# Layer 1 of a four-layer graph network: the copy of the attention weights becomes a job of its own and moves ahead of the norm and the scatters, and the attention product moves ahead of the aggregation

## The chip, the cores and the metric

The kernel runs on one core of one Trainium2 chip. The metric is device time in microseconds (us). Three runs of the kernel before gave 2053.06, 2053.97 and 2055.26 us; 2053.97 is their median.

## What is computed

The input `x` is 128 graphs of 64 nodes with 256 features; `adj` is one 64x64 adjacency matrix that all graphs share. Four graph layers follow one another. Each is added to its input and normalised over the features:

```python
x = _layernorm(x + _L0(x, adj, W, a))
x = _layernorm(x + _L1(x, W_lin, W_val, a, W_out, adj, src, dst))
x = _layernorm(x + _L2(x, adj, W1, b1, g1, be1, W2, b2, g2, be2))
x = _layernorm(x + _L3(x, adj, Wg0, bg0, Wg1, bg1, Wih, Whh, bih, bhh))
```

The change sits in the second half of layer 1 and in the first operation of layer 2. They are, in short:

```python
# layer 1: attention along 512 edges (src -> dst), 4 heads of 64
Xq = (H @ W_lin.T).reshape(bt, n, h, dh)
Xv = (H @ W_val.T).reshape(bt, n, h, dh)
e = einsum('behd,hd->beh', leaky_relu(Xq[:, src] + Xq[:, dst], 0.2), a)
e = e + log(A0[src, dst] + EPS)
ex = exp(e - segment_max(e, src)[src])        # softmax over the edges of one src
attn = ex / segment_sum(ex, src)[src]
Y = segment_sum(attn * Xv[:, dst], src)
return Y @ W_out.T
# layer 2
agg = einsum('nm,bmd->bnd', A_hat, features)  # A_hat: adjacency, scaled by degrees
h = relu(batchnorm(agg @ W1.T + b1))          # statistics over all 8192 rows
return batchnorm(h @ W2.T + b2)
```

Layer 0 is a graph attention with a dense 64x64 softmax. Layer 3 has two graph convolutions and then four LSTMs; it takes the larger part of the time, and the change doesn't touch it.

## The kernel before

**Tiling.** The 8192 rows are cut into NQ = 16 blocks of 512 rows, which is eight graphs or PQ = 4 chunks of 128 rows (two graphs each). A block stays on the chip in a tile `A` from layer to layer.

**The loop of layer 1.** It runs over `q` from 0 to 15. Each step is cut into eight sub-steps `b`. A sub-step starts with `l1_graph`, which is one graph: the product L355 forms queries plus keys on the 512 edges in `z`, and ScalarE's L357 copies them to `u` with a relu. After it come the jobs that the table `between` lists for this sub-step. They belong to neighbouring blocks:

- Layer 0 of the blocks q+1 and q+2 (`l0_a` to `l0_e`). The change's neighbours in it are ScalarE's copy of the transposed attention `eT` (L285) and the product L293, which has eight weight loads and reads `eT`.
- `l1_t` and `l1_qv`: the transposes, the query product (L318), the value product (L321), and the copies out of their banks. ScalarE's L328 copies `qs`, VectorE's L329 subtracts for the other half, ScalarE's L330 copies to `spad`, and ScalarE's L331 copies the values `v`.
- `sums`: the reduction over heads (L346), which reads `u`.
- The softmax of a pair of blocks, numbered S, every second step. `l1_softmax` runs L365 to L375 with the exponential L374, and `l1_sums` holds the two scans L380 and L381. `l1_weights` transposes (L389), normalises (L397), writes the weights with four scatters of GpSimd's into a table in memory (L401), and loads the table back as `ld` with two DMAs on SyncE's queue.
- `v_a` of a block LAG = 3 steps back. GpSimd's copy L414 sorts the weights of this block out of `ld` into `am`. Then comes the attention product L422, 64 matmuls of 64x64, and two copies of ScalarE's (L426) empty its banks into `yT`.
- `v_b`: the output product L436, the residual sum of VectorE's (L438), the layernorm, and a store of the result. In the layernorm, VectorE takes statistics (L95, L96) and adds the epsilon (L85), GpSimd raises to the power -1/2 (L86), VectorE negates the mean (L98), and GpSimd scales the four chunks (L100).
- `v_c`: the aggregation of layer 2 (L456, 64 matmuls of 64x64 on the normalised rows) and the copy into `A` (L460 in the loop, two L463 after it).

**What sets the order.** In the loop the helper `step` chains only TensorE's instructions of successive jobs. All other engines get an order from a scheduler, which places what is ready. After the loop the helper `given` holds every job behind the one before it on TensorE, VectorE, ScalarE and GpSimd alike. Each engine works through its queue in the order that was built.

**Buffers.** A PSUM bank comes from `bank`: three of the name `m` go round among most products, two are `z`, one is `e`. The tiles `am`, `ld`, `y`, `at` and `yT` have one buffer each, so a new one waits for the last reader of the old one. `v` has five buffers.

**The end of layer 1.** After the loop the blocks 12 to 15 are still under way. The list `fill` holds pieces of layer 2's first product (`up_block`, with the matmuls L749, ScalarE's L754 and VectorE's statistics L755; later pairs of blocks with L820). A piece is put after every job `v_a`, `v_b` and `v_c`. The last softmax (S = 7) belongs to the blocks 14 and 15: its `l1_softmax` comes right after the loop, its `l1_sums` and `l1_weights` among the first pieces.

Of the kernel before, what the change touches and what calls it, by code (L numbers as in the profile page):

```python
# [8 lines left out]
F32 = mybir.dt.float32  # L9
# [8 lines left out]
P = 128  # L18
NB = 128
N = 64  # L20
D = 256
KD = D // P
HEADS = 4
# [3 lines left out]
NQ = 16  # L27
PQ = 4
# [13 lines left out]
def kernel(ctx: ExitStack, tc: tile.TileContext, i, out):  # L42
# [67 lines left out]
    def given(do, *args, **more):  # L110
        traced = nc.cur_bb.bb.instructions
        first = len(traced)
        with ExitStack() as order:
            for e in latest.values():
                order.enter_context(tc.issue_after(e))
            r = do(*args, **more)  # L116
        for t in traced[first:]:
            if t.engine in (mybir.EngineType.PE, mybir.EngineType.DVE, mybir.EngineType.Activation,
                            mybir.EngineType.Pool):
                latest[t.engine] = t  # L120
        return r
# [8 lines left out]
    with ExitStack() as two:  # L130
# [7 lines left out]
        vp = values.enter_context(tc.tile_pool(name="vp", bufs=1, side="right"))  # L138
# [5 lines left out]
        def bank(shape, name="m", bufs=3):  # L144
            return (psm if name == "m" else ps).tile([P] + shape, F32, name=name, bufs=bufs)
# [158 lines left out]
        L1 = {}  # L304
# [102 lines left out]
                nc.sync.dma_start(ld[S][s * N:(s + 1) * N], half)  # L407


        def v_a(q):  # L410
            S, b = divmod(q, BPS)
            v = L1[q]["v"]
            am = vp.tile([P, PQ * HEADS, N], F32, name="am")
            nc.gpsimd.tensor_copy(am.rearrange("p (e r) n -> p e r n", e=2),  # L414
                                  ld[S].rearrange("p n (e b r) -> p b e r n", e=2, b=BPS)[:, b])
            pY = [bank([KD, PQ, N]) for _ in range(2)]
            for c in range(PQ):
                for h in range(HEADS):
                    for s in range(2):
                        r = slice(s * N, (s + 1) * N)  # L420
                        r0 = (h % 2) * 64
                        nc.tensor.matmul(pY[s][r0:r0 + 64, h // 2, c, :], v[r, c, h * 64:(h + 1) * 64],  # L422
                                         am[r, (c % 2) * 2 * HEADS + c // 2 * HEADS + h, :], start=True, stop=True)
            yT = L1[q]["yT"] = vp.tile([P, KD, PQ, 2, N], F32, name="yT")
            for s in range(2):
                nc.scalar.activation(yT[:, :, :, s, :], pY[s], AF.Copy)  # L426
# [234 lines left out]
        LAG = BPS + 1  # L661
# [4 lines left out]
        def step(do, n, *more):  # L666
            if not 0 <= n < NQ:
                return
            traced = nc.cur_bb.bb.instructions
            first = len(traced)  # L670
            if queue:
                with tc.issue_after(queue[-1]):
                    do(n, *more)
            else:
                do(n, *more)
            mine = [t for t in traced[first:] if t.engine == mybir.EngineType.PE]
            queue.extend(mine[-1:])
# [4 lines left out]
        for q in range(NQ):  # L682
            S = q // BPS - 1 if q % BPS == 0 else -1
            between = [
                [(l0_e, q + 1), (l0_a, q + 2)],
                [(sums, q if q else -1), (l1_softmax, S)],
                [(l1_sums, S), (l0_b, q + 2)],
                [(v_b, q - LAG - 1)],
                [(l1_weights, S), (l1_t, q + 1), (l0_c, q + 2)],
                [(sums, q), (l1_qv, q + 1, 0)],  # L690
                [(v_c, q - LAG - 1), (v_a, q - LAG)],
                [(l0_d, q + 2), (l1_qv, q + 1, 1)],
            ]
            for b in range(GQ):
                step(l1_graph, q, b)
                for do, n, *more in between[b]:
                    step(do, n, *more)
                if setup:
                    setup.pop(0)()
        sums(q)  # L700
        S = NQ // BPS - 1
# [55 lines left out]
        def up_block(q):  # L757
            for m in range(2):
                put(q, m, up(q, m))
                if m == 0:  # L760
                    last_tail()
            pz = [up(q, m) for m in (2, 3)]
            for m in (2, 3):
                put(q, m, pz[m - 2])
# [134 lines left out]
        def tile_sums(b):  # L899

            t2, t3, t4 = rooms[next(rooms_at) % len(rooms)]
            t1 = b(0, 1)
            given(nc.gpsimd.tensor_tensor, t3, b(1, 1), t1, OP.subtract)
            given(nc.vector.tensor_sub, t1, t1, b(0, 0))
            given(nc.gpsimd.tensor_tensor, t2, b(1, 1), t1, OP.subtract)
            given(nc.gpsimd.tensor_tensor, t4, b(1, 0), t2, OP.subtract)
            return [t1, t2, t3, t4]
# [12 lines left out]
        def inputs(q):  # L920
            return lambda k, n: Aq(q + n)[:, k * QT:(k + 1) * QT]

        def up_job(q, g, T, done=None, feed=iter(()), **more):
            a = lambda m, k: w1[:, k, (2 * g + m) * P:(2 * g + m + 1) * P]
            dst = lambda m, n: hidden(q + n, 2 * g + m)
            stats = lambda m, n: nc.vector.bn_stats(st1[:, 2 * g + m, q + n, :], dst(m, n))
            seven(Seven([(a, [SW[0][:, n, g] for n in range(4)], inputs(q), T)],
                        lambda m: b1[:, 2 * g + m:2 * g + m + 1], dst, stats, done, **more), feed)
# [3 lines left out]
        def one(q):  # L932
            return lambda: up_block(q)

        def pair(q, g):
            return lambda: up_job(q, g, T[q])

        fill = [one(n) for n in range(7)] + [pair(n, g) for n in (7, 9) for g in range(2)]
        given(v_b, NQ - LAG - 1)
        fill.pop(0)()  # L940
        given(l1_sums, S)
        fill.pop(0)()
        given(v_c, NQ - LAG - 1, False)
        given(l1_weights, S)
        sums_at = {3: 7, 5: 9}
        for n, (do, q) in enumerate([(do, q) for q in range(NQ - LAG, NQ) for do in (v_a, v_b, v_c)]):
            given(do, q, *[False] * (do == v_c))
            fill[n]()
            if n in sums_at:
                T[sums_at[n]] = tile_sums(inputs(sums_at[n]))  # L950
        q = NQ - LAST - 1
# [1023 lines left out]
```

## Time and profile before

| what | value |
|---|---|
| median of three runs | 2053.97 us (2053.06 to 2055.26) |
| profiled execution | 2051.53 us, of which its span is 2049.7 us |
| granted TensorE clock, mean | 0.986 |
| 0 to 155 us | TensorE busy 125.81 |
| 155 to 520 us (365.0) | TensorE 342.48, ScalarE 239.62, VectorE 212.96, GpSimd 136.50 |
| 520 to 620 us (100.0) | TensorE 95.51, VectorE 54.88, GpSimd 43.59, ScalarE 35.68 |
| 620 to 2049.7 us (1429.7) | TensorE 1379.77, VectorE 895.54, GpSimd 672.64, ScalarE 625.24 |

The profile is one execution, recorded by the hardware. Its span reaches from the first to the last instruction; the execution's own time is a little longer. The engines are PE (TensorE's matmuls), PEld (its weight loads), DVE (VectorE), ACT (ScalarE), POOL (GpSimd) and SP (SyncE, which issues DMAs). A line of the timeline gives start, length, engine, program line, operation, and output and input tiles with shapes; a bracket at its end says how long the engine had been idle and which instruction ended that. A line of the waits gives the waiting tile and line, the instruction that released it, the total, how often, and the longest. The four stretches of the table are the start with layer 0, the loop with softmax and attention, the end of layer 1, and layers 2 and 3.

### The profile page before, as it was taken

The page shows a single profiled execution, that of the slowest core. Times are in us where ns is not written, and L with a number is a line of the kernel's source. Part 1 is how long each engine was busy: PE and PEld are TensorE (multiplying, and loading weights), DVE is VectorE, ACT ScalarE, POOL GpSimd, SP SyncE. Part 2 cuts the span into 40 slices and gives each one's busy share as a digit, 9 for nine tenths or more (in the row PEclk, how much of TensorE's full clock was granted, in tenths as well). Part 3 has the DMA queues.
Part 4 walks back from the last instruction along what each step waited for, and adds up shares of the span by engine and source line. Part 5 has one row for each costly group of instructions (what it writes and reads, how often), then busy time and mean ns, then how long its engine had stood idle before and what let it go on. Part 6 is the DMA issues. An engine that isn't in the chain of part 4 may idle for free.

```text
span 2049.7 us, 31505 instructions
## 1 busy us (share of the span) xinstructions
PE 1943.6 (95%) x11447; PEld 1332.9 (65%) x11447; DVE 1256.3 (61%) x2763; ACT 987.6 (48%) x1892; POOL 883.8 (43%) x1017
## 2 busy tenths in 40 slices
PE   5999999999899989899999999999999999999997
PEld 4666667766454435477677477677577667578685
DVE  7456665564457454765566865556775557764566
ACT  2766667666335633634343644343544333544333
POOL 1123334343345543564545543435443445444264
PEclk8999999999999999999999999999999999999998
DMA  5344443332112125432242243132143032131022
GB/s 134 79 65 68 79 69 54 66 50 39 37 29 60 41 103 171 158 136 98 112 143 85 77 140 139 42 126 91 52 153 120 21 113 65 44 119 78 0 65 70
DMA packets 236539, 173.84 MB, mean 85 GB/s; under 512 B 150624, under 2 KB 213600, under 8 KB 233056
## 3 DMA queue, kind: packets, MB, share of 16 engines
q1 hardware_dynamic: 234528, 169.86, 29.1%
q8 instruction: 90, 1.47, 0.3%
q0 software_dynamic: 1024, 1.05, 0.2%
q10 hardware_dynamic: 832, 0.92, 0.1%
q14 instruction: 65, 0.53, 0.1%
HBM read 110.18 MB, written 61.60 MB: 84 GB/s over the span
## 4 chain that ended last, share of the span: by engine, by line
PE 68%; DVE 17%; ACT 5%; POOL 4%; issue 4%; DMA 1%; SPq 0%; DVEq 0%; POOLq 0%; ACTq 0%
PE l L1700 25%; PE l L1656 7%; PE l L1437 4%; PE pz L820 4%; PE e L346 3%; PE m L318 2%; PE pz L749 2%; PE g L1336 2%; PE m L253 2%; PE m L321 2%; PE z L355 2%; PE pz L1017 2%; PE g L1324 2%; DVE ln_st L95 1%; DVE cell L1614 1%
## 5 line engine op out<-in xcount | busy, mean ns | idle before, releaser
L1700 PE MATMUL l<-xs,wx 128*128 128x256 f32 (+1 forms) x896 | 277.0, 400 | 5.7 <-DVE gate L1719 4.2
L1700 PE MATMUL l<-hs,wh 128*128 128x256 f32 (+1 forms) x896 | 276.5, 399 | 2.9 <-DVE hs L1564 2.1
L1715 ACT ACTIVATE kept<-l 128x256 f32<-128x256 f32 (+1 forms) x224 | 88.6, 402 | 332.2 <-PE l L1700 330.7
L86 POOL TENSOR_TENSOR ln_rs<-ln_rs,mhalf 128x2 f32<-128x2 f32 (+2 forms) x98 | 86.4, 882 | 338.1 <-DVE ln_rs L98 334.9
L1700 PE MATMUL l<-H,wx 128*128 128x256 f32 (+1 forms) x672 | 210.5, 402 | 4.3 <-DVE gate L1728 3.4
L1700 PE MATMUL l<-hid,wh 128*128 128x256 f32 (+1 forms) x672 | 208.8, 399 | 0.0
L1700 PEld LDWEIGHTS l<-xs,wx 128*128 128x128 f32 x896 | 168.6, 190 | 50.7 <-issue 5.8
L1700 PEld LDWEIGHTS l<-hs,wh 128*128 128x128 f32 x896 | 169.2, 190 | 46.8 <-DVE hs L1564 4.7
L1733 ACT ACTIVATE gate<-gate,bias 128x512 f32<-128x512 f32 (+1 forms) x280 | 170.6, 657 | 42.0 <-DVE gate L1724 34.8
L1656 PE MATMUL l<-H,wx 128*128 128x256 f32 (+5 forms) x672 | 185.2, 431 | 4.9 <-DVE H L116 2.7
L1656 PEld LDWEIGHTS l<-H,wx 128*128 128x128 f32 x672 | 118.8, 190 | 65.5 <-issue 34.2
L357 ACT ACTIVATE u<-z 128x1024 f32<-128x1024 f32 x128 | 130.3, 1025 | 63.4 <-PE z L355 62.6
L1700 PEld LDWEIGHTS l<-H,wx 128*128 128x128 f32 x672 | 125.7, 190 | 42.6 <-DVE gate L1728 7.4
L1700 PEld LDWEIGHTS l<-hid,wh 128*128 128x128 f32 x672 | 127.2, 190 | 32.0 <-issue 2.6
L1723 POOL TENSOR_TENSOR gate<-gate,kept 128x256 f32<-128x256 f32 (+1 forms) x84 | 64.9, 773 | 154.2 <-DVE kept L1721 153.9
L329 DVE TENSOR_TENSOR qs<-m,qs 64x256 fp32r<-64x256 f32 x128 | 54.1, 422 | 109.1 <-ACT qs L328 107.0
L355 PE MATMUL z<-gath_r,qs 128*128 128x512 f32 x256 | 99.9, 478 | 0.6 <-ACT u L357 0.4
L1622 ACT ACTIVATE gate<-cell 128x512 f32<-128x512 f32 (+1 forms) x88 | 58.6, 666 | 86.5 <-DVE cell L1614 64.5
L1568 POOL TENSOR_TENSOR hs<-hid 128x256 f32<-128x256 f32 (+1 forms) x28 | 27.4, 977 | 168.3 <-DVE hid L1600 85.2
L1728 DVE TENSOR_TENSOR gate<-l,gate 128x256 f32<-128x256 f32 (+1 forms) x112 | 50.0, 446 | 61.4 <-POOL gate L1723 36.4
L1610 POOL TENSOR_TENSOR cell<-gate,cell 128x512 f32<-128x512 f32 (+1 forms) x56 | 75.4, 1367 | 28.4 <-ACT gate L1733 28.4
L1717 DVE TENSOR_TENSOR gate<-l,kept 128x256 f32<-128x256 f32 (+1 forms) x112 | 49.2, 439 | 57.1 <-ACT gate L1733 32.9
(375 smaller groups left out, 4095.3 us busy)
## 6 DMA issues: line engine op xcount, KB each, us to landing
wx<-sums SPq DMA_DIRECT2D x9, 2048.0 KB
wh<-sums SPq DMA_DIRECT2D x9, 1792.0 KB
way<-st SPq DMA_DIRECT2D x54, 256.0 KB
st<-way SPq DMA_DIRECT2D x216, 64.0 KB
xin<-in_x SPq DMA_DIRECT2D x16, 512.0 KB
ld<-table SPq DMA_DIRECT2D x16, 512.0 KB
x_dram<-y SPq DMA_DIRECT2D x16, 512.0 KB
x2r<-x_dram SPq DMA_DIRECT2D x32, 256.0 KB
```

The lines of the kernel that those rows point to most:

```text
L86: nc.gpsimd.tensor_tensor(dst, dst, mhalf[:, :n], OP.pow)
L346: nc.tensor.matmul(pes[S][n * CG:(n + 1) * CG, :], apad[:, k, CG - HEADS - r0:2 * CG - HEADS - r0], u[:, k, :], start=r0 == 0 and k == 0, ...
L355: nc.tensor.matmul(z[:, k, :], L1[q]["qs"][c][:, s, k * P:(k + 1) * P], gath_r, start=True, stop=True)
L357: nc.scalar.activation(u, z, AF.Relu)
L820: nc.tensor.matmul(self.bank[at], lhs, rhs, start=first and n == 0, stop=n == len(self.terms) - 1, skip_group_check=True)
L1437: nc.tensor.matmul(self.bank[at], lhs, rhs, start=new, stop=True, skip_group_check=True)
L1610: nc.gpsimd.tensor_tensor(c, t, c, OP.mult)
L1656: nc.tensor.matmul(b, w.raw[0][:, k, at, m, :], x, start=k == 0, stop=k == KD - 1)
L1700: nc.tensor.matmul(self.banks[j], lhs, rhs, start=src == 0, stop=src == 1)
L1715: nc.scalar.activation(self.keep(j), b, AF.Copy)
L1723: e.tensor_tensor(t[0][:, 1], t[0][:, 1], k[5], OP.add)
L1733: given(lambda: nc.scalar.activation(dst, dst, f, bias=b))
```

## The change

`v_a` is split. The new function `v_m` holds GpSimd's copy of the weights, and `v_a` keeps the attention product; the tile goes from one to the other by the dictionary `L1[q]`.

In the loop `v_m` of a block is called three sub-steps earlier than its product, just before `v_b` of the block before it. In sub-step 6 `v_a` now comes before `v_c` of the block before it.

After the loop, the last softmax's `l1_sums` comes before `v_b` of block 12 and before the first piece of `fill`. The copy of block 13 and the last softmax's `l1_weights` come before the second piece and before `v_c` of block 12. The copies of the blocks 14 and 15 come right after the attention product of the block before.

The diff:

```diff
@@ -407,12 +407,14 @@
-        def v_a(q):
+        def v_m(q):
             S, b = divmod(q, BPS)
-            v = L1[q]["v"]
-            am = vp.tile([P, PQ * HEADS, N], F32, name="am")
+            am = L1[q]["am"] = vp.tile([P, PQ * HEADS, N], F32, name="am")
             nc.gpsimd.tensor_copy(am.rearrange("p (e r) n -> p e r n", e=2),
                                   ld[S].rearrange("p n (e b r) -> p b e r n", e=2, b=BPS)[:, b])
+
+        def v_a(q):
+            v, am = L1[q]["v"], L1[q]["am"]
             pY = [bank([KD, PQ, N]) for _ in range(2)]
@@ -685,10 +687,10 @@
                 [(l0_e, q + 1), (l0_a, q + 2)],
                 [(sums, q if q else -1), (l1_softmax, S)],
                 [(l1_sums, S), (l0_b, q + 2)],
-                [(v_b, q - LAG - 1)],
+                [(v_m, q - LAG), (v_b, q - LAG - 1)],
                 [(l1_weights, S), (l1_t, q + 1), (l0_c, q + 2)],
                 [(sums, q), (l1_qv, q + 1, 0)],
-                [(v_c, q - LAG - 1), (v_a, q - LAG)],
+                [(v_a, q - LAG), (v_c, q - LAG - 1)],
                 [(l0_d, q + 2), (l1_qv, q + 1, 1)],
             ]
@@ -936,15 +938,18 @@
         fill = [one(n) for n in range(7)] + [pair(n, g) for n in (7, 9) for g in range(2)]
+        given(l1_sums, S)
         given(v_b, NQ - LAG - 1)
         fill.pop(0)()
-        given(l1_sums, S)
+        given(v_m, NQ - LAG)
+        given(l1_weights, S)
         fill.pop(0)()
         given(v_c, NQ - LAG - 1, False)
-        given(l1_weights, S)
         sums_at = {3: 7, 5: 9}
         for n, (do, q) in enumerate([(do, q) for q in range(NQ - LAG, NQ) for do in (v_a, v_b, v_c)]):
             given(do, q, *[False] * (do == v_c))
+            if do == v_a and q + 1 < NQ:
+                given(v_m, q + 1)
             fill[n]()
```

## The prediction

> **What bounds the kernel now.** I read the page first (shares, chain that ended last), then the waits of TensorE, then the timeline, once inside the layer-1 loop and once over its end.
>
> ```profile
> PE 1943.6 (95%) x11447; PEld 1332.9 (65%) x11447; DVE 1256.3 (61%) x2763; ACT 987.6 (48%) x1892; POOL 883.8 (43%) x1017
> ...
> PE 68%; DVE 17%; ACT 5%; POOL 4%; issue 4%; DMA 1%; SPq 0%; DVEq 0%; POOLq 0%; ACTq 0%
> ```
>
> TensorE is busy for 95% of the span and carries 68% of the chain, so a change of order pays only through TensorE's idle time. Between 155 and 520 us (the steps of the loop that hold the moved code) the view by stretches gives it 342.5 busy of 365.0; between 520 and 620 us (the end of layer 1) 95.5 of 100. The waits that the change aims at:
>
> ```profile
> PE m L318 <- ACT yT L426: 5.4, 10, 0.6
> ...
> PE m L422 <- POOL am L414: 3.9, 2, 2.5
> ```
>
> The columns are total us, times, longest. The query product (L318) waits ten times for the copy that empties the attention product's bank; the attention product (L422) waits twice for GpSimd's copy of the weights. In the loop, one step looks like this (start, length, engine):
>
> ```profile
> 278.52 0.60 ACT L331 ACTIVATE v<-m 128x512 f32<-128x512 f32 x1
> ...
> 279.21 1.16 PEld L422 LDWEIGHTS m<-am,v 64*64 64x64 f32 x64
> ...
> 280.57 1.03 ACT L460 ACTIVATE A<-z 128x1024 f32<-128x1024 f32 x1
> ...
> 281.49 1.08 ACT L426 ACTIVATE yT<-m 128x512 f32<-128x512 f32 x2
> ...
> 284.03 0.74 PEld L318 LDWEIGHTS m<-wq,tT 128*128 128x128 f32 x4 [0.29 <-ACT eT L285]
> ...
> 286.08 0.60 ACT L331 ACTIVATE v<-m 128x512 f32<-128x512 f32 x1 [0.16 <-PE m L321]
> 286.11 1.72 PEld L293 LDWEIGHTS m<-wh,eT 128*128 128x128 f32 x8
> ...
> 286.57 0.15 ACT L330 ACTIVATE spad<-m 64x4 f32<-64x4 f32 x1
> 286.74 0.38 ACT L328 ACTIVATE qs<-m 64x256 fp32r<-64x256 f32 x1
> ```
>
> See that ACT runs without a gap from 278.52 to the end of eT, that L422 starts just after the value copy (L331) has emptied its bank, and that L293's eight loads at 286.11 run in one piece. The end of layer 1, GpSimd first, then TensorE:
>
> ```profile
> 545.80 1.09 POOL L401 DMA_INDIRECT table<-at,place  x1 [10.42 <-DVE at L397]
> ...
> 554.57 0.96 POOL L401 DMA_INDIRECT table<-at,place  x1 [1.92 <-DVE st L755]
> ...
> 567.65 2.16 POOL L100 TENSOR_SCALAR y<-y,ln_rs 128x256 f32<-128x256 f32 x4
> ```
>
> ```profile
> 516.57 1.16 PE L422 MATMUL m<-am,v 64*64 64x64 f32 x64 [1.41 <-POOL am L414]
> ...
> 557.49 1.16 PE L422 MATMUL m<-am,v 64*64 64x64 f32 x64 [2.50 <-POOL am L414]
> ...
> 568.25 2.07 PE L456 MATMUL m<-aht,y 64*64 64x64 f32 x64 [0.80 <-POOL y L100]
> ...
> 573.02 1.16 PE L422 MATMUL m<-am,v 64*64 64x64 f32 x64
> ```
>
> Two idle stretches sit here: 2.50 us before block 13's attention product, behind four scatters, and 0.80 plus a stretched L456 (2.07 for 1.16) for block 13's normalised rows. And the load of the table: issued at 318.33 in the loop, its copy starts at 328.71 after 1.10 us of waiting for it, so 10.4 us; other loop loads take 9.2 to 10.9.
>
> **What the Trainium skill says.** "PSUM — Partial Sum Buffer", section "Engine vs sequencer instructions": ScalarE's, VectorE's and GpSimd's queues are strict first-in-first-out and matmuls start in program order. The trace agrees (the L422 wait of 2.50 us holds all matmuls behind it), and the argument rests on it. Same page, "PSUM bank collisions raise a hardware error": two engines are kept apart per bank. Here L330 follows DVE's L329 on the same bank (DVE ends 284.67, L330 starts 284.70). "DMA: Bandwidth & Descriptors", "Specifications": below 512 B a transfer is under line rate; the table load has 128 B rows, and 0.5 MB of it kept the engines busy in two bursts from 559 to 567 us.
>
> **The change part by part.** It adds and removes no instruction. The built orders of both kernels, set side by side per engine, show four real differences; the SP queue differs only in a few early input loads. In the loop GpSimd's order is the same as before: there the copy already stood ahead.
>
> A. *Attention product ahead of the aggregation, loop steps 4 to 14.* L422 would move from 279.21 to 278.29, but its first bank is the value copy's, free at 278.52+0.60 = 279.12. So it starts at 279.2 as before, L456's 1.02 us now stands between it and L355, and L318 starts at about 282.3 instead of 282.13. The bank wait of L318 goes. Next late: its second half at 284.03, which waits for eT. Between 280.57 and 284.0 ACT does the same copies in another order (1.03+1.08+1.05+0.63), so eT ends when it did. TensorE arrives some 0.1 us early instead of 0.29. Cost 0.0, bounds -0.1 and +0.2 per step. If ACT's cover were gone, it would be the 0.2. In odd steps the same holds (second half at 316.78, after eT).
>
> B. *A by-product in the same steps: ACT copies the values later.* In the new build L331 stands behind both L330s and the last L328 of its group. The second of these L330s needs DVE's L329 pair (285.29+0.88 = 286.17): 286.20, then L328 at 286.38, then L331 at about 286.79, ending 287.39 instead of 286.68. L293's fifth load (of eight, 0.215 each) needs that bank: due at 286.11+4x0.215 = 286.97, now 287.43. Stall about 0.45. What follows on TensorE (L355, L346, and every second step L365, which starts the softmax chain on DVE) is released by TensorE itself, so nothing takes it back. L293 follows in ten of these steps (4 to 13): 10x0.45 = +4.5. Bounds: +1.5 if most of it falls into later waits, +5.5 for 0.55 each.
>
> C. *Last loop step, 15.* The copy of the weights ends at 516.51, in the same place on GpSimd. Before, L456 (513.1 to 515.1) filled the wait; now it stands behind L422, and L355, u and L346 follow it by its 1.05 us: +1.05 (0.9 to 1.2).
>
> D. *End of layer 1.* Clock of the profile, C left out. The last softmax's sums (L380, L381) now follow L374 directly: exp ends 528.2, the two scans 1.21+1.40, so 530.9; then two L438 of 0.69, statistics and two L755, L98 at about 535.9. GpSimd: L86 1.05, L100 2.2 to 3.5, so block 12's rows at 539.8. TensorE reaches them at 526.1+6.9+1.0+6.9 = 541.0 (eight L749 as sixteen passes of 0.43, transposes, eight more): covered by 1.2 us, and the sums cost nothing. The weights copy of block 13 ends 541.8; L422 waits at most for ACT's L463, 0.75 us: the 2.50 goes.
> What is late next: GpSimd's queue now holds four scatters, then block 14's copy, then block 13's L86 and L100. Scatters from 541.8, the fourth 8.77 later (545.80 to 554.57), its landing 2.14 after that (316.19 to 318.33): the table load starts at 552.7. Landing 10.0 later (9.2 to 10.9): 562.7. Copy 1.95, L86 1.05, first L100 0.6: L456 of block 13 starts at 566.5. TensorE, with the product (1.1), sixteen L749 (13.8) and L436 (3.45), is there at 561.3: about 5 us idle where there were 0.8. Then L456 2.07 and eight L749 6.9: block 14's product at 575.5. It was at 573.02 after the same work, so +2.5. Bounds 0.0 and +5.5, from the load's spread, L100's (2.2 to 3.5) and one us in the DVE list. Later copies and tile sums on GpSimd have over 5 us to spare.
>
> Sum: 0.0+4.5+1.05+2.5 = +8.05. Against the profiled execution: 2051.53 (span 2049.7 and 1.8 around it) gives 2059.6. That execution lay 2.4 below the median of the runs, so I put the sum on the median: 2053.97+8.05 = 2062.0.
>
> **Rivals.** *1, the waits go and nothing comes instead:* the 5.4 of L318 and the 2.50 are gained, C paid: 2053.97-5.4-2.5+1.05 = 2047.1. It needs eT to end 0.5 earlier (before 283.5), though ACT has no gap there, and the table load to land before 557; against it the unbroken ACT line. *2, the loop hides B:* C and D alone, +3.55, 2057.5. For it, waits of 0.5 to 1 us on other engines' results every second step; against it, that these are released by TensorE. *3, the GpSimd line is longer:* load at 10.9, L100 at 3.5, and B at 0.55: 2053.97+5.5+1.2+5.5 = 2066.2. For it, the load's own spread.
>
> **How the numbers follow.** Forecast (slower by about 8) 0.70; rival 1 0.07; rival 2 0.15; rival 3 0.08. A run of this kernel can tell 0.2%, 4.1 us, from no change; rival 2 lies inside, and a little of the forecast's lower edge. Faster 0.07, same 0.16, slower 0.77. The sum of the lower bounds that I hold likely (B 1.5, C 0.9, D 0) is +2.4, 2056.4; the upper 2066.2. Range 2056 to 2066.5; rival 1 and the outer edges stay outside.
>
> **What would show it.** A: L422 waits for L331 (m bank), L318 no longer for L426. B: L293 waits about 0.45 for L331 in ten steps, and the period of two steps (the copies L414 that start at 280.63 and 341.88, 61.25 apart) grows by 0.9. C: L346 after the last step waits for u by a microsecond more. D: no long wait before L422 at 542, one of about 5 us before L456 at 561, released by GpSimd's L100, with its copy waiting for the table. Wrong would be an L293 without a wait, or a table load that lands within 6 us.

## The result and the profile after

The changed kernel was slower: 2066.0 us median (2063.47 to 2068.53) beside 2054.48, a ratio of 1.0060 with a 95% interval of 1.0047 to 1.0072, or +12 us. A second measurement gave 1.0031 (1.0020 to 1.0042), +6.4 us. The sum of the prediction was +8.05. The profiled execution took 2064.54 us, its span 2062.7, 13.0 more than the span before. Executions of one kernel scatter by several us, so the time of one profile is not the median of its kernel.

Waits of TensorE in the changed kernel, from 90 to 700 us (total us, times, longest), and below them the same for its weight loads:

```profile
PE m L424 <- ACT v L331: 6.7, 11, 0.9
PE m L458 <- POOL y L100: 5.2, 1, 5.2
...
PE m L424 <- POOL am L413: 3.8, 1, 3.8
```

```profile
PEld m L293 <- ACT v L331: 5.4, 11, 0.7
```

L422 is now L424, L456 is L458. The wait of L318 for yT (5.4 us in ten) is gone. The product waits for the value copy instead (one of the eleven waits was there before), L293 waits for it too (11 times; one of 0.7 was there before), and the aggregation of block 13 waits 5.2 us for its normalised rows. In the loop, the timeline of after shows L293 so:

```profile
350.72 0.17 ACT L330 ACTIVATE spad<-m 64x4 f32<-64x4 f32 x1 [0.28 <-DVE qs L329]
350.85 2.24 PE L293 MATMUL m<-wh,eT 128*128 128x256 f32 x8
350.90 0.38 ACT L328 ACTIVATE qs<-m 64x256 fp32r<-64x256 f32 x1
351.31 0.60 ACT L331 ACTIVATE v<-m 128x512 f32<-128x512 f32 x1
...
351.96 0.73 PEld L293 LDWEIGHTS m<-wh,eT 128*128 128x128 f32 x4 [0.48 <-ACT v L331]
```

L331 stands behind the last L330 and L328, ends at 351.91, and only then does L293's fifth load start. The last loop step, and GpSimd and TensorE at the end of layer 1:

```profile
524.13 1.98 PE L424 MATMUL m<-am,v 64*64 64x64 f32 x64 [3.81 <-POOL am L413]
525.89 1.68 PE L458 MATMUL z<-aht,y 64*64 64x64 f32 x64
```

```profile
560.14 0.96 POOL L401 DMA_INDIRECT table<-at,place  x1 [1.92 <-DMA table<-at,place]
572.65 1.91 POOL L413 COPY am<-ld 128x1024 f32<-128x1024 f32 x1 [11.55 <-DMA ld<-table]
574.52 1.05 POOL L86 TENSOR_TENSOR ln_rs<-ln_rs,mhalf 128x4 f32<-128x4 f32 x1
575.68 2.17 POOL L100 TENSOR_SCALAR y<-y,ln_rs 128x256 f32<-128x256 f32 x4
```

```profile
576.29 2.32 PE L458 MATMUL m<-aht,y 64*64 64x64 f32 x64 [5.24 <-POOL y L100]
578.54 8.71 PE L751 MATMUL pz<-A,w 128*128 128x512 f32 x16
```

The line of GpSimd is the one that the prediction drew: the fourth scatter, then a copy that waits 11.55 us for the table, then block 13's norm. But the matmuls behind these waits are longer than before: the two products of the last loop step take 1.98 and 1.68 us (1.16 is their length elsewhere), sixteen passes of L751 (layer 2's first product, L749 before) take 8.71 (7.03 at 564.02). The view by stretches says why. Columns: stretch, its length, busy time of PE, PEld, DVE, ACT and POOL with their counts, granted TensorE clock, DMA share, GB/s.

```profile
571.50:574.90 3.40, 0.00 (x0) 0.00 (x0) 0.84 (x2) 0.28 (x1) 2.25 (x2) 1.00 0.02 4
574.90:578.30 3.40, 2.01 (x63) 1.95 (x64) 0.00 (x0) 0.00 (x0) 2.85 (x5) 0.50 0.00 0
578.30:581.70 3.40, 3.40 (x16) 1.64 (x12) 0.00 (x0) 1.08 (x2) 0.00 (x0) 0.50 0.41 153
581.70:585.20 3.50, 3.50 (x9) 1.52 (x8) 1.31 (x2) 1.38 (x2) 0.00 (x0) 0.99 0.01 6
```

After a stretch without matmuls, TensorE's clock is granted at half speed for two stretches of 3.41 us, called windows below. The same happens inside the loop of this execution, where before it didn't. First after, then before, at the same transposes (L227, L264):

```profile
237.00:240.40 3.40, 1.73 (x13) 1.26 (x13) 3.37 (x10) 1.29 (x3) 0.00 (x0) 1.00 0.71 69
240.40:243.80 3.40, 3.40 (x17) 1.02 (x18) 2.96 (x9) 1.03 (x1) 3.14 (x4) 0.50 0.03 10
```

```profile
238.20:241.60 3.40, 2.06 (x16) 1.43 (x14) 3.33 (x10) 1.62 (x2) 0.00 (x0) 1.00 1.34 187
241.60:245.00 3.40, 2.92 (x22) 1.48 (x26) 3.37 (x13) 1.62 (x2) 1.71 (x2) 1.00 0.20 31
```

I cut each profile at four landmarks of TensorE: the second, seventh and eighth L365, and the first L820 (their lines shift with the edits). The table gives the lengths in us, in brackets how much of each ran at half clock.

| kernel | start | loop, 10 steps | last steps | end of layer 1 | rest |
|---|---|---|---|---|---|
| before | 168.0 | 306.2 (0) | 47.5 (6.8) | 70.9 (0) | 1457.1 |
| after | 164.1 | 317.1 (10.2) | 50.4 (10.2) | 75.2 (6.8) | 1456.0 |
| after_again | 168.0 | 311.0 (0) | 49.8 (10.2) | 75.6 (6.8) | 1455.9 |
| copy_only | 168.1 | 306.3 (0) | 47.6 (6.8) | 72.6 (3.4) | 1455.7 |
| loop_only | 167.0 | 311.0 (0) | 49.0 (6.8) | 72.6 (3.4) | 1455.7 |
| loop_vfirst | 166.6 | 307.9 (0) | 49.3 (10.2) | 70.9 (0) | 1454.9 |
| loop_vfirst15 | 165.2 | 309.6 (3.4) | 47.4 (6.8) | 72.6 (3.4) | 1455.6 |
| tail_only | 166.5 | 306.3 (0) | 47.4 (6.8) | 75.2 (6.8) | 1456.2 |
| tail_fill | 164.1 | 306.2 (0) | 49.5 (13.1) | 72.7 (0.5) | 1456.0 |
| tail_fix | 167.9 | 306.4 (0) | 49.3 (12.4) | 67.8 (1.2) | 1455.9 |
| fill15 | 166.1 | 306.4 (0) | 48.0 (6.8) | 67.2 (0) | 1457.2 |
| fill_waits | 166.3 | 306.4 (0) | 44.9 (0) | 67.2 (0) | 1457.4 |
| fetch_shift | 185.8 | 310.6 (0) | 50.2 (13.6) | 72.6 (3.4) | 1457.2 |

The three middle columns of after are 18.1 us longer than those of before. The start and the rest, where the change moves next to nothing, give back 3.9 and 1.1, which leaves the 13.0 of the spans. The start of after ran at half clock for 13.7 us, that of before for 23.9.

### The profile page after: what moved, and what is told of

Its sections match the earlier page's. It is cut to its first block, busy times and chain, and to the rows that moved or that the text cites. A ratio compares the mean times of both kernels' runs of the same rounds, so it can differ in the third digit from the quotient of the medians.

```text
span 2062.7 us, 31500 instructions
## 1 busy us (share of the span) xinstructions
PE 1948.6 (94%) x11447; PEld 1336.6 (65%) x11447; DVE 1256.7 (61%) x2763; ACT 988.7 (48%) x1892; POOL 884.6 (43%) x1017
## 3 DMA queue, kind: packets, MB, share of 16 engines
q0 software_dynamic: 1024, 1.05, 0.2%
## 4 chain that ended last, share of the span: by engine, by line
PE 66%; DVE 18%; ACT 7%; POOL 4%; issue 4%; DMA 1%; DVEq 0%; SPq 0%; POOLq 0%; ACTq 0%
PE l L1705 26%; PE l L1661 7%; PE pz L822 4%; PE l L1442 4%; PE e L346 3%; PE g L1341 2%; PE pz L751 2%; PE pz L1022 2%; PE m L253 2%; PE g L1329 1%; PE z L355 1%; DVE cell L1619 1%; ACT qs L328 1%; PE l L1510 1%; PE m L318 1%
## 5 line engine op out<-in xcount | busy, mean ns | idle before, releaser
L86 POOL TENSOR_TENSOR ln_rs<-ln_rs,mhalf 128x2 f32<-128x2 f32 (+2 forms) x98 | 86.6, 884 | 335.4 <-DVE ln_rs L98 329.6
L355 PE MATMUL z<-gath_r,qs 128*128 128x512 f32 x256 | 101.3, 484 | 0.1
```

The costliest lines, as they stand in the source:

```text
L86: nc.gpsimd.tensor_tensor(dst, dst, mhalf[:, :n], OP.pow)
L355: nc.tensor.matmul(z[:, k, :], L1[q]["qs"][c][:, s, k * P:(k + 1) * P], gath_r, start=True, stop=True)
```

## Experiments

**The moved copy alone: copy_only.** The loop calls the copy early, nothing else is changed.

```diff
-                [(v_b, q - LAG - 1)],
+                [(v_m, q - LAG), (v_b, q - LAG - 1)],
```

> Only the loop's copy of the weights (GpSimd) is called three sub-steps earlier; the product stays behind the aggregation and the end of layer 1 is as before. The built order of every engine is that of the kernel before. Theory 1 (the loss in the loop comes with the swap of L424 and L458, which lets ScalarE's value copy L331 slide back): ratio 1.000, within 2 us of before. Theory 2 (the earlier copy itself costs, by its am buffer or GpSimd's queue): +5 us or more. As a second profile of the old order it also tells about the half-clock stretches of TensorE: if it depends on chance where the 3.41 us windows of the clock fall, then the waits before L227 and L264 (0.66+0.69+0.48 us every second step) give half-clock windows in some steps of this execution, none in others, and its time less the lost clock stays at about 2020 us.

Measured: 0.9999 (0.9991 to 1.0008). The earlier call in the loop moves no instruction and costs nothing. No half-clock window fell into the loop here either: the expected chance hits did not come, and the four windows around L227 were 0.60 to 0.61 busy, as in the profile before.

**The parts: loop_only and tail_only.** loop_only has the changed kernel's table `between` and the old end of layer 1, with each copy directly ahead of its product. tail_only is the reverse.

loop_only against the changed kernel:

```diff
-        given(l1_sums, S)
         given(v_b, NQ - LAG - 1)
         fill.pop(0)()
-        given(v_m, NQ - LAG)
-        given(l1_weights, S)
+        given(l1_sums, S)
         fill.pop(0)()
         given(v_c, NQ - LAG - 1, False)
+        given(l1_weights, S)
...
+            if do == v_a:
+                given(v_m, q)
             given(do, q, *[False] * (do == v_c))
-            if do == v_a and q + 1 < NQ:
-                given(v_m, q + 1)
```

tail_only against the changed kernel:

```diff
-                [(v_m, q - LAG), (v_b, q - LAG - 1)],
+                [(v_b, q - LAG - 1)],
...
-                [(v_a, q - LAG), (v_c, q - LAG - 1)],
+                [(v_c, q - LAG - 1), (v_m, q - LAG), (v_a, q - LAG)],
```

> The loop as in the changed kernel, the end of layer 1 as before. Theory 1: steps 4 to 13 lose 0.45 to 0.6 us each at L293 (its fifth load behind L331), the last step loses 1.05 because L458 no longer fills the wait for am: +5.5 to +7 us at full clock, and 2 to 7 us of half-clock windows on top, so 2060 to 2067, with L424 waiting for L331 some ten times and an L293 wait in place of L318's wait for yT. Theory 2 (all the loss is made at the end of layer 1): within 2 us of before.

Measured: 1.0038 (1.0024 to 1.0051), +7.8 us; the waits in the loop are those of after. Its profile has no half clock in the ten steps of the loop, and they take 311.0 us against 306.2: +4.8.

> The end of layer 1 as in the changed kernel, the loop as before. Theory 1: the 2.50 us before block 13's product go, about 5 us before block 13's aggregation come, released by L100 behind a copy that waits for the table load: +2.5 us at full clock, and two half-clock windows after that wait stretch what follows by 1.8 us: +4 in all, 2058. Theory 2 (the end of layer 1 gains, and only the loop costs): -2.5 us, 2051.5.

Measured: 1.0015 (1.0008 to 1.0021), +3.1 us. Block 13's product has no wait, its aggregation waits 4.80 us, and 6.8 us behind it run at half clock. So both parts of the change lose, the loop more.

**The value copy put back: loop_vfirst.** In loop_only, ScalarE's L331 of each second half block is held ahead of the last L330s and L328.

```diff
                     for s in range(2):
...
+                        if c == 3 and s == 0:
+                            nc.scalar.activation(v[:, 2 * c2:2 * c2 + 2, :], pv, AF.Copy)
+                            held.enter_context(tc.issue_after(nc.cur_bb.bb.instructions[-1]))
                         nc.scalar.activation(sp[r, s, c % 2, 0, q % BPS, c // 2, :], pq[r, D:], AF.Copy, scale=SLOPE)
-            nc.scalar.activation(v[:, 2 * c2:2 * c2 + 2, :], pv, AF.Copy)
+            if c2 == 0:
+                nc.scalar.activation(v[:, 2 * c2:2 * c2 + 2, :], pv, AF.Copy)
```

> As loop_only, but in the second half of every block ScalarE's value copy L331 is held ahead of the last L330s and the last L328, where it stood in the kernel before. Theory 1 (the late L331 makes L293's fifth weight load wait 0.47 us, net 0.3 us a step from step 4 to 13): those waits vanish, 3 us less than loop_only, so before +4 to +5: what is left is the last step's L458 (1.05 us and a half-clock window) and the 1.4 us for which TensorE stands inside L458 in step 7. Theory 2 (the swap on TensorE itself costs, by the later L355): no gain against loop_only, before +8.

Measured: 1.0010 (1.0001 to 1.0019), +2.1 us, a larger gain over loop_only (5.7) than the 3 expected; the profile has 3.1 of it. The two runs belong to different series, each beside its own runs of before, so I rest on the profiles here. In the timeline of loop_vfirst L293's eight loads run in one piece again:

```profile
347.65 1.71 PEld L293 LDWEIGHTS m<-wh,eT 128*128 128x128 f32 x8
```

The loop falls from 311.0 to 307.9. So L293's ten waits are worth 3.1 us, and the 0.47 of each counts as 0.3 at the next L355.

**The last step put back: loop_vfirst15.** As loop_vfirst, with the order of the two products reversed in step 15.

```diff
-                [(v_a, q - LAG), (v_c, q - LAG - 1)],
+                [(v_a, q - LAG), (v_c, q - LAG - 1)][::1 if q < NQ - 1 else -1],
```

> As loop_vfirst, and in the last loop step the aggregation L458 stands ahead of the product L424 again, so that it fills the wait for am. Theory 1: the last step takes 1.0 us less at full clock and up to 1.7 us less by the clock; before +1 to +3 remains, with the waits of steps 4 to 14 at L424 for L331 (0.6 each) instead of L318's for yT, which cost nothing. Theory 2 (the swap itself costs in every step): before +5 or more.

Measured: 1.0008 (1.0001 to 1.0014), +1.6 us, over the runs not told apart from loop_vfirst. In the profile the last steps take 47.4 as before instead of 49.3. The ten waits of L424 for L331 in steps 4 to 13 are still there, and cost next to nothing. What is left in the loop, 307.9 at full clock against 306.2, is nearly all one stop, inside an L458 (L463 in this kernel's lines) of step 7:

```profile
277.50 1.14 PE L463 MATMUL z<-aht,y 64*64 64x64 f32 x62
280.06 0.27 PE L463 MATMUL z<-aht,y 64*64 64x64 f32 x1 [1.42 <-issue]
```

Nothing in the view releases it. All five profiles with the swap of that step have it at the same, last matmul (1.34 to 1.56 us), and copy_only does not.

**Where the stop comes from: fetch_shift.** As loop_vfirst15, with 47 more small matmuls in the setup.

```diff
-            nc.tensor.matmul(pd[:, 0:1], an, ones[:, 0:1], start=True, stop=True)
+            for _ in range(48):
+                nc.tensor.matmul(pd[:, 0:1], an, ones[:, 0:1], start=True, stop=True)
```

> As loop_vfirst15, with one small matmul of the setup (64 rows, one column) repeated 47 times, so that TensorE's instructions behind it lie elsewhere in the 16 KB packets in which they are loaded. Theory 1 (the 1.4 us for which TensorE stands inside L458 in step 7 are a wait for such a packet, which in every profile with the swap begins just as that run of 256 short instructions does): the wait is gone from step 7, the stretch from the second to the seventh L365 takes 306.3 to 306.6 us at full clock instead of 307.9. Theory 2 (it belongs to something in step 7, GpSimd's copy that starts at the same time): it stays before the last L458 of step 7.

Measured: 1.0100 (1.0084 to 1.0116). The start takes 20 us longer, so only the loop is of use. The 306.3 to 306.6 us expected there did not come: it takes 310.6. Yet the stop has left step 7, and one of its size stands in step 9, behind the last matmul of that step's L458:

```profile
363.72 0.30 PEld L360 LDWEIGHTS z<-gath_r,qs 128*128 128x128 f32 x2 [1.69 <-ACT A L467]
```

The view names the copy L467, but it ended at 363.29, and in other steps L360 starts before that copy does. The trace's DMA records have a 16 KB instruction packet that begins at 361.02, within that run of short instructions, 2.70 us before TensorE goes on. In the five profiles with the stop in step 7 one begins likewise, 2.25 to 2.61 us before (280.33 in loop_only). In copy_only it begins at 275.35, three microseconds ahead of the run. So the stop is not tied to step 7 or to GpSimd's copy in it. That it moves with the place of the instructions in the stream, and is a wait for such a packet, fits the six profiles that have it; nothing more direct was tried, so this is not shown. The smaller stops of 0.4 us in five other steps of fetch_shift were not followed up.

**The norm ahead of the copy: tail_fix.** As tail_only, but the copies of blocks 14 and 15 follow `v_b` of the block before.

```diff
-            if do == v_a and q + 1 < NQ:
+            if do == v_b and q + 1 < NQ:
```

> The end of layer 1 as in tail_only, but block 14's (and 15's) copy of the weights stands behind the norm of the block before it instead of ahead; loop as before. Theory 1 (the norm of block 13 waits in GpSimd's queue behind a copy that waits for the table): no wait before block 13's aggregation, so the 2.50 us, the 0.80 us and the stretched L456 (0.9) of before are gained: -4 us, 2050, and no half-clock window between 560 and 590 us. Theory 2 (block 13's norm is late for another reason, the scatters or VectorE's list): a wait of 2 us or more before it stays, and the time is not below before by more than 1 us.

Measured: 0.9981 (0.9972 to 0.9990), -3.9 us. In GpSimd's timeline the norm of block 13 now precedes the copy that waits for the table:

```profile
559.99 2.17 POOL L100 TENSOR_SCALAR y<-y,ln_rs 128x256 f32<-128x256 f32 x4
564.70 1.97 POOL L413 COPY am<-ld 128x1024 f32<-128x1024 f32 x1 [2.54 <-DMA ld<-table]
```

```profile
563.61 1.16 PE L458 MATMUL m<-aht,y 64*64 64x64 f32 x64
571.76 1.16 PE L424 MATMUL m<-am,v 64*64 64x64 f32 x64
```

Neither product waits; the end of layer 1 takes 67.8 instead of 70.9. So the moves up to the copy of block 13 were a gain (the 2.50 us wait is gone), and the place of block 14's copy lost it again.

**The clock: tail_fill.** As tail_only, with useless work in the 4.8 us wait.

```diff
+            if do == v_c and q == NQ - LAG:
+                for m in range(2):
+                    given(up, 0, m)
             given(do, q, *[False] * (do == v_c))
```

> As tail_only, with two products of layer 2's first weights (eight matmuls, 3.5 us) computed once more and thrown away, just before block 13's aggregation, where TensorE stands idle for 4.8 us. Theory 1 (after a 3.41 us window in which TensorE was nearly idle its clock runs at half speed for one or two windows): the wait shrinks to about 1.3 us, the half-clock window behind it goes, L458 takes 2.1 us at most and the four products after it 7.0 instead of 8.7: 1.5 to 2 us faster than tail_only although TensorE has 3.5 us more to do. Theory 2 (the half clock is not tied to this wait): the same time as tail_only or slower by up to 3.5 us, with half-clock windows at the same place.

Measured: 1.0004 (0.9996 to 1.0013) where tail_only had 1.0015. Over the runs the two intervals just overlap; what follows rests on one profile of each. tail_only first, then tail_fill:

```profile
564.48 2.31 PE L458 MATMUL m<-aht,y 64*64 64x64 f32 x64 [4.80 <-POOL y L100]
566.72 9.10 PE L751 MATMUL pz<-A,w 128*128 128x512 f32 x16
```

```profile
563.86 2.07 PE L458 MATMUL m<-aht,y 64*64 64x64 f32 x64 [0.84 <-POOL y L100]
565.86 7.13 PE L751 MATMUL pz<-A,w 128*128 128x512 f32 x16
```

3.5 us more work, no half clock behind it, and the end of layer 1 is 2.5 us shorter. What a wait costs here is the wait and the slow matmuls after it. The last steps of the same profile are 2.1 us longer than in tail_only, with 13.1 us at half clock instead of 6.8; the filler comes after them.

**The changed kernel again: after_again.** No edit.

> The changed kernel once more, beside the same runs of before as the others. Theory 1: its loss against before is that of loop_only (7.9 us) and tail_only (3.1 us) together, +11; its time at full clock (span less half of the half-clock windows) is again 2027 to 2031, whatever the number of half-clock windows, and these fall elsewhere in the loop than in the first profile. Theory 2 (the two parts of the change get in each other's way): more than +14 or less than +8.

Measured: 1.0031 (1.0020 to 1.0042), +6.4 us. That is below the +8 set as the limit between the theories (the interval reaches +8.6). The profiled execution, 2062.14 us, was the slowest of the seven; its parts are those of loop_only and tail_only: 311.0 and 75.6. There is no half clock in the loop, where the first profile had three windows. Span less half of the half-clock time is 2028.3, against 2028.8 in the first. The median execution had a mean clock of 0.989, that of before beside it 0.987, so the clock hid some of the loss here.

**Filling more waits: fill15 and fill_waits,** both from tail_fix. The first computes block 11's aggregation twice in step 15, the second also repeats transposes of two softmaxes.

```diff
-            for c in range(PQ):
+            for c in list(range(PQ)) * (2 if q == NQ - LAG - 2 else 1):
...
+                if row is e and S in (0, 6):
+                    for c in list(range(EC)) * 4:
+                        nc.tensor.transpose(p_[:, c, :], row[:, c * P:(c + 1) * P], ident)
```

> As tail_fix (the loop of before, the end of layer 1 of the change with the copies of blocks 14 and 15 behind the norms), with the aggregation L458 of block 11 in the last loop step computed twice into the same bank, 1.1 us of useless work where TensorE then waits 1.4 us for am. Theory 1 (a 3.41 us window of the clock in which TensorE is busy for less than about 0.55 is followed by one at half speed): the window at 514 to 518 us, 0.56 busy in tail_fix and followed by two half-clock windows, becomes over 0.8 busy, the half clock from 518 to 525 us goes, and the profile from the seventh L365 to the eighth takes 47 us or less instead of 49.3; over the runs, where that window sometimes escapes, 0.5 to 3 us faster than tail_fix. Theory 2 (half clock not set by the idle share): no faster, and slower by up to 1.1 us.

Measured: 0.9978 (0.9969 to 0.9987), not told apart from tail_fix. The half clock from 518 us is gone in its profile, but the window ahead of it was 0.58 busy, not over 0.8, and the last steps took 48.0 us where 47 or less was expected, so this shows little.

> As fill15, and the transposes L389 of the exponentials of the softmaxes S = 0 and S = 6 repeated four times more into the same bank (1.8 us each of useless work), where TensorE waits 2.2 us for the tile dn and every profile shows one or two half-clock windows afterwards (at 121 to 129 and 483 to 491 us). Theory 1: these windows go too: 3 to 6 us faster than fill15, 2040 to 2043 us where before has 2050.5. Theory 2: no gain, or a loss of up to 3.6 us.

Measured: 2043.86 us, 0.9957 (0.9943 to 0.9970), -9 us: faster than both kernels. The median missed the expected 2040 to 2043, but before was slower beside it as well, at 2052.8. fill15 first, then fill_waits, at the wait for `dn` of S = 6:

```profile
478.00:481.40 3.40, 1.16 (x7) 0.48 (x5) 3.31 (x5) 1.56 (x2) 0.86 (x2) 1.00 0.00 0
481.40:484.80 3.40, 2.60 (x11) 2.23 (x12) 3.40 (x9) 0.60 (x1) 0.00 (x0) 0.50 0.00 0
```

```profile
480.10:483.50 3.40, 2.25 (x18) 1.62 (x16) 3.37 (x11) 0.60 (x1) 0.00 (x0) 1.00 0.00 0
483.50:486.90 3.40, 3.36 (x24) 1.53 (x25) 2.71 (x7) 1.51 (x2) 3.09 (x5) 1.00 0.02 5
```

With the repeats the stretch is 2.25 of 3.40 busy and full clock stays; the last steps take 44.9 us instead of 48.0. At the other repeat, S = 0, the half-clock window of fill15 at 123 us is gone too, but the start takes 166.3 us, 166.1 in fill15. The repeats also let the scheduler move some work of the other engines, so not all of the gain need be the clock's.

## Why the prediction was right and wrong

**A** held: L424 waits for L331, by 0.90 us in every second step (the forecast's times make 0.83) and by 0.27 in the others. Apart from the stop in step 7, the swap costs next to nothing in steps 4 to 14: in loop_vfirst15 the loop at full clock, less that stop, is 0.2 us longer than before.

**B** held as a mechanism: L331 slid back, and L293 waits for it in ten more steps, 4.7 us in all against 4.5. "What follows on TensorE ... is released by TensorE itself, so nothing takes it back" was wrong by a third: 0.47 of wait became 0.3. The ten steps still lost 4.8, because 1.4 us came from the stop in step 7, which no row of the profile before showed. That the two nearly made up for each other was luck.

**C** was named right and mis-sized. "+1.05 (0.9 to 1.2)" counts TensorE at full clock. The last steps lost 1.5 to 2.9 us in the three profiles of loop_only and after; in the two of after, 10.2 us of them run at half clock where before had 6.8, one window of it right behind the wait of 3.8 us for am.

**D**: the order on GpSimd, the load's landing and the wait ("about 5 us", measured 5.24) came as written. The copy started at 572.65, 22.6 us after the first scatter where the sum had 20.9. The fourth scatter is 1.3 of that: it came 10.10 us after the first instead of 8.77, because the third waited 3.25 for VectorE's L757. TensorE reached its wait later too, 21.0 us after the first scatter where the sum had 19.5, so the length of the wait came out right partly by luck. (Copy, L86 and the first L100 add up to 3.6 us, where the prediction goes on with 3.8; 3.64 was measured. The exponential before the sums is L375; L374 subtracts the maximum ahead of it.) The term "+2.5" measured +4.3 and +4.7 in the two profiles of after. Of the 4.3, 0.25 is L458 at 2.32 for 2.07, and 1.68 is L751 at 8.71 for 7.03, both by the half clock; without them +2.4.

The step that failed is "Sum: 0.0+4.5+1.05+2.5 = +8.05": it has no term for the clock. The profile before ran at full clock through the ten steps and through the end of layer 1, and I priced each new wait by its length alone. In the first profile of after 27 us ran at half clock between the second L365 and the first L820, before 6.8. In the loop that came in one execution and not in the other, while the waits at L227 and L264 were there in both. So a single sum could not give both measurements.

The runs show what the clock does to them. The eleven executions of after have spans from 2052.5 us at a mean clock of 0.990 to 2066.8 at 0.982, and the two go together (correlation -0.97). Span times mean clock takes off half of all half-clock time; that is rough, since a wait in such a window loses nothing. It comes to 2030.1 us in the median of the first measurement of after and 2030.2 in the second, beside 2022.0 for before in the second: +8.2, near the +8.05. But after ran at a median clock of 0.989 there, and before at 0.987, so only +6.4 was left. In the first measurement after ran at 0.982 to 0.985, and +12 came out; of before's runs there only the profiled one has its clock on record, 0.986. So at full clock the sum was nearly right, in part by the luck told under B. That it lies between the two measurements is luck as well.

Why before's loop is spared is argued, not shown. Two of its steps take 61.25 us, 17.95 windows of 3.413, so that the short idle time at L227 falls on nearly the same place of the window each time, which was 0.60 to 0.61 busy. Two steps of after at full clock take 62.2, 18.2 windows, so the place can shift. In the first profile of after it was 0.51, 0.51, 0.70 and 0.52 busy, and half clock followed all but the third; in after_again and loop_only the emptiest windows of the loop were 0.57 and 0.58 busy, and no half clock followed.

Rival 1 is out: both waits went, and others came. Rival 2 is out: loop_only alone loses 7.8, and 4.8 of it stand in the ten steps of its profile. Rival 3 had nearly the time of the first measurement (2066.2), but not by its cause: the line on GpSimd was 1.7 us longer than the sum had it, through the scatters and not through the load's landing (10.31) or L100 (2.17), and the wait came out at 5.24 all the same.

## What to carry to other kernels

Price a new wait of TensorE together with what follows it: if it leaves a clock window half empty, the next one can run at half speed, and useless matmuls in the wait can be a gain (3.5 us of them in tail_fill, 1.8 in fill_waits; the 1.1 of fill15 showed none). When a job is moved ahead in one queue, look at what now stands behind it: the early copy of block 13 paid, the same move of block 14's put a norm behind a copy that waits for a DMA. And when only TensorE's order is fixed, compare the built order of ScalarE too; a copy that slides back by two small instructions cost 3 us here.

## What the runs showed of the hardware

The half-clock stretches came in lengths of 3.41 us or multiples of it. I cut ten profiles (all but fill15, fill_waits and fetch_shift) from 90 to 700 us into windows of that length, set on the changes of the clock, and took the share in which matmuls were busy in each window at full clock:

| busy share of a window | windows | followed by half clock |
|---|---|---|
| under 0.45 | 28 | 28 |
| 0.45 to 0.53 | 7 | 6 |
| 0.53 to 0.58 | 12 | 2 |
| over 0.58 | 1685 | 0 |

The Trainium skill, "TensorE: Matmul & The Clock Gate", section "Part 1: The HAM clock gate", has the free-running window of 3413 ns and the half rate after an idle window. The traces agree with both, and show besides that a window needn't be idle: about half empty was enough here. Between 0.45 and 0.58 both outcomes occur, so no exact limit is shown.

TensorE's stop of 1.3 to 1.6 us in or behind a run of 256 short instructions was the other surprise. Its times fit a wait for an instruction packet, which isn't shown directly. A mere reordering brought it about, and the profile names no releaser for it, or one that had already been done.
